# Attention of a two-layer graph network: scores of two heads at a time, alternating between the row halves of the array

## The chip, the cores and the metric

The kernel runs on one core of one Trainium2 chip. The metric is the device time in microseconds; the times of the runs shown are 4495.94, 4510.7 and 4512.44 us, with the median 4510.7. All arithmetic is fp32. In the profile PE is TensorE's matrix product, PEld its load of the stationary operand, DVE is VectorE, ACT is ScalarE, POOL is GpSimd and SP is SyncE.

## The reference

Sixteen graphs of 1024 nodes with 256 channels share one adjacency matrix. Layer 0 is an attention whose queries come from a weighted graph product, layer 1 a graph convolution with two batch norms. Cut to what matters:

```python
h = relu(layernorm(x))
Wg = adj * A_s(mean over channels of h)          # per graph, 1024 x 1024
q = relu(einsum(h^T, Wg) * para)                 # 4 heads of 64 channels
k, v = split(h @ kv_w)
attn = softmax(q @ k^T * scale)                  # per graph and head, 1024 x 1024
x = x + attn @ v
h = relu(layernorm(x))
agg = A_hat @ h                                  # normalised adj + I
y = relu(batchnorm(agg @ W1^T + b1))             # over all graphs and nodes
x = x + batchnorm(y @ W2^T + b2)
```

## The kernel before

The first part of the kernel runs graph by graph. `pre(b)` makes queries, keys and values of graph b; `post(b)` is layer 1 of graph b up to the statistics of its first batch norm, with `y` going to DRAM. The second part, after all graphs, applies the batch norms and the second product; the change doesn't touch it.

Queries and keys lie in SBUF with channels on the partitions: two tiles of 128 partitions for 256 channels, so that each tile holds two heads, one on partitions 0 to 63 and the other on 64 to 127 (tile `k`, first partition `r0`). Attention is cut into units of one graph, one head and 128 queries: 16 x 4 x 8 = 512 units, in the order graph, head, query tile.

`scores` of a unit makes two products of 64 rows by 512 keys (line 262) into one PSUM tile of two banks (`sc`, from a pool of two tiles), takes the row maximum on VectorE (line 270), the exponential with its sum on ScalarE (line 272, into `p`), and the reciprocal of the sum (line 273). A product of 64 rows uses only the half of the array whose rows belong to those partitions. `attend` of a unit transposes `p` on TensorE in eight blocks (line 283, `tp`), copies each four blocks to SBUF, the first on ScalarE (line 288) and the second on VectorE (line 290), multiplies with the values (line 295, `po`, eight products), and adds the scaled result to `x` on VectorE (line 303).

In the program, `scores` of unit i+1 stands ahead of `attend` of unit i. Between the units stands other work: `background(b)` gives out, in 46 pieces spread over the units of graph b, `post(b-1)` (products `pa` line 319 and `py` line 332, normalisation `h_b` line 154 on ScalarE) and then `pre(b+1)` (transposes `cbp` line 108 and `htp` line 198, graph weights `w` lines 176 to 184 on ScalarE and VectorE, products `pg` line 213, `pk` line 231, `pv` line 247). Graph 0 has the preparation of the adjacency matrix in place of `post`; the last graph has no `pre`, so the later part of its attention stands alone. When a graph's pieces run out, attention runs alone too.

The order on each engine is fixed when the program is built, and it isn't the program's: the framework moves instructions ahead of others that it expects to wait. So a score product can stand among the transposes and products of an earlier unit. At run time each engine works through its list in order; TensorE's weight loads may run beside the product in front of them.

## Time and profile before

| | |
|---|---|
| times of the runs shown | 4495.94, 4510.7, 4512.44 us (median 4510.7) |
| span of the profiled execution | 4498.9 us |
| its own time, beside the span | the page gives the span alone; the median of the runs is 11.8 us above it |
| mean granted TensorE clock | 0.96 |
| attention with its background | 80 to 4104 us of the span |
| score products `sc`, line 262, busy | 1146.5 us in 2048 passes |
| weighted sums `po`, line 295, busy | 1086.4 us in 8192 passes |
| transposes `tp`, line 283, busy | 564.3 us in 4096 |
| DMA | mean 33 GB/s |

A product of fp32 operands stands in the trace as two passes, a transpose as one. Lengths of TensorE's records overlap (each reaches to its modelled end), so what a pass holds the engine for is read from one start to the next. A value in brackets on a timeline's line is idle time of that engine just before it and what ended it. The granted clock is 1.00 or 0.50 in any short stretch; a mean between the two says how much of the stretch was spent at each.

### The profile page before, as it was taken

How to read it: one execution, taken by the hardware profiler on the slowest of the kernel's cores; microseconds unless marked ns; L12 is line 12 of the kernel's file. 1: busy time of each engine (PE TensorE's matmuls, PEld its weight loads, DVE VectorE, ACT ScalarE, POOL GpSimd, SP SyncE). 2: the span in 40 equal slices, each digit the busy share in tenths (PEclk: the TensorE clock that was granted, in tenths of full speed). 3: DMA queues.
4: the chain of work that ended last, by engine and by line, in shares of the span. 5: the costliest groups of instructions: out<-in, count | busy, mean ns of one | idle time of the engine just before them, and what ended most of it. 6: DMA issues, size and time to landing. Idle time of an engine off the chain costs nothing.

```text
span 4498.9 us, 48480 instructions
## 1 busy us (share of the span) xinstructions
PE 4345.1 (97%) x19848; PEld 2752.5 (61%) x19848; DVE 1842.1 (41%) x3314; ACT 1705.9 (38%) x3075; POOL 159.9 (4%) x237
## 2 busy tenths in 40 slices
PE   6999999999999999999999999999999999999994
PEld 5765757566665757566665756666575756655443
DVE  5343334344443444444433434344333444333344
ACT  4434334252433434343433434243433425232443
POOL 0000000000000000000000000000000000000001
PEclk9799999999999999999999999999999999999997
DMA  2000010000000000000001000000000000000537
GB/s 112 1 19 19 1 38 1 29 10 19 19 10 29 1 33 6 29 10 19 19 1 38 1 29 10 22 17 15 24 1 36 3 29 10 10 19 29 191 140 271
DMA packets 44236, 148.34 MB, mean 33 GB/s; under 512 B 3824, under 2 KB 20720, under 8 KB 35824
## 3 DMA queue, kind: packets, MB, share of 16 engines
q1 hardware_dynamic: 27120, 78.13, 4.8%
q0 software_dynamic: 16896, 67.12, 3.9%
q8 instruction: 157, 2.57, 0.2%
q14 instruction: 63, 0.52, 0.0%
HBM read 78.13 MB, written 67.11 MB: 32 GB/s over the span
## 4 chain that ended last, share of the span: by engine, by line
PE 90%; ACT 5%; DMA 2%; issue 1%; DVE 1%; POOL 0%; POOLq 0%; SPq 0%; DVEq 0%; ACTq 0%
PE po L295 23%; PE sc L262 21%; PE tp L283 10%; PE pg L213 10%; PE pa L319 10%; PE pz L413 5%; PE py L332 5%; PE pk L231 2%; PE pv L247 2%; ACT w L176 2%; ACT h_b L154 1%; DMA xo<-x_d 1%; DMA out_dram<-xo 1%; ACT p L272 1%; PE htp L198 1%
## 5 line engine op out<-in xcount | busy, mean ns | idle before, releaser
L295 PEld LDWEIGHTS po<-v,pt 128*128 128x128 f32 x8192 | 1015.9, 199 | 450.9 <-ACT pt L288 306.1
L262 PE MATMUL sc<-k,q 64*128 64x512 f32 x2048 | 1146.5, 649 | 35.6 <-ACT p L272 35.6
L295 PE MATMUL po<-v,pt 128*128 128x64 f32 x8192 | 1086.4, 285 | 14.9 <-ACT pt L288 8.1
L288 ACT COPY pt<-tp 128x512 f32<-128x512 f32 x512 | 297.9, 582 | 1308.5 <-PE tp L283 1306.9
L270 DVE TENSOR_REDUCE smx<-sc 128x1 f32<-128x1024 f32 x512 | 625.7, 1222 | 366.0 <-PE sc L262 360.0
L283 PEld LDWEIGHTS tp<-ident,p 128*128 128x128 f32 x4096 | 455.3, 143 | 310.3 <-issue 164.3
L272 ACT ACTIVATE p<-sc,smx 128x1024 f32<-128x1024 f32 x512 | 568.7, 1111 | 166.2 <-DVE smx L270 111.4
L283 PE MATMUL tp<-ident,p 128*128 128x128 f32 x4096 | 564.3, 279 | 0.8 <-ACT p L272 0.8
L262 PEld LDWEIGHTS sc<-k,q 64*128 64x128 f32 x2048 | 314.8, 187 | 337.5 <-issue 262.9
L213 PE MATMUL pg<-w,h_a 128*128 128x256 f32 x2048 | 500.1, 400 | 8.5 <-DVE q L221 5.4
L319 PE MATMUL pa<-aht,h_b 128*128 128x512 f32 x1024 | 481.4, 629 | 4.1 <-ACT h_b L154 4.1
L303 DVE SCALAR_TENSOR_TENSOR x<-po,smx,x 128x64 f32<-128x64 f32 x512 | 145.1, 283 | 769.4 <-PE po L295 769.4
L213 PEld LDWEIGHTS pg<-w,h_a 128*128 128x128 f32 x2048 | 400.4, 201 | 63.4 <-issue 5.4
L290 DVE COPY pt<-tp 128x512 f32<-128x512 f32 x512 | 349.1, 682 | 55.0 <-PE tp L283 55.0
L319 PEld LDWEIGHTS pa<-aht,h_b 128*128 128x128 f32 x1024 | 204.7, 204 | 245.9 <-issue 240.3
L176 ACT ACTIVATE w<-cbc,csum 128x256 f32<-128x256 f32 x512 | 227.1, 499 | 163.0 <-PE pg L213 162.5
L332 PE MATMUL py<-at,w 128*128 128x512 f32 x512 | 250.0, 608 | 0.0
L413 PE MATMUL pz<-yin,w 128*128 128x512 f32 x512 | 221.9, 597 | 11.1 <-ACT yin L407 11.1
L340 ACT ACTIVATE y<-py,vec 128x512 f32<-128x512 f32 x128 | 87.9, 687 | 308.3 <-PE py L332 211.3
L273 DVE RECIPROCAL smx<-smx 128x1 f32<-128x1 f32 x512 | 82.7, 161 | 270.6 <-ACT p L272 268.5
L326 DVE COPY at<-pa 128x512 f32<-128x512 f32 x64 | 44.3, 692 | 345.0 <-PE pa L319 345.0
L221 DVE TENSOR_TENSOR q<-pg,para_sb 128x256 f32<-128x256 f32 x128 | 54.0, 424 | 316.3 <-PE pg L213 315.2
(71 smaller groups left out, 2213.7 us busy)
## 6 DMA issues: line engine op xcount, KB each, us to landing
y_d<-y POOLq DMA_DIRECT2D x128, 256.0 KB, 2.7
yin<-y_d SPq DMA_DIRECT2D x32, 1024.0 KB, 4.8
x<-in_x_dram SPq DMA_DIRECT2D x16, 1024.0 KB, 5.5
x_d<-x POOLq DMA_DIRECT2D x16, 1024.0 KB, 4.1
xo<-x_d SPq DMA_DIRECT2D x16, 1024.0 KB, 7.7
out_dram<-xo POOLq DMA_DIRECT2D x16, 1024.0 KB, 7.1
adj_sb<-in_adj_dram SPq DMA_DIRECT2D x1, 4096.0 KB, 15.2
aht<-in_adj_t_dram SPq DMA_DIRECT2D x1, 4096.0 KB, 25.1
```

Of the source, the lines that this page charges most:

```text
L176: nc.scalar.activation(w[:, t, :], cbc[:, q * QW : (q + 1) * QW], AF.Abs, bias=csum[:, t : t + 1], scale=-1.0,)
L213: nc.tensor.matmul(pg[:, :QW], h[:, t, k * P : (k + 1) * P], w[:, t, :], start=(t == 0), stop=(t == NT - 1),)
L262: nc.tensor.matmul(sc[:, g * FB : (g + 1) * FB], qs[b][k][r0 : r0 + HD, t * P : (t + 1) * P], ks[b][k][r0 : r0 + HD, g * FB : (g + 1) * FB ...
L270: nc.vector.tensor_reduce(sm[:, 0:1], sc, AX.X, ALU.max, negate=True)
L272: nc.scalar.activation(pr, sc, AF.Exp, bias=sm[:, 0:1], accum_out=sm[:, 1:2])
L283: nc.tensor.transpose(tp[:, j * P : (j + 1) * P], pr[:, m * P : (m + 1) * P], ident)
L288: nc.scalar.copy(pt, tp)
L290: nc.vector.tensor_copy(pt, tp)
L295: nc.tensor.matmul(po[:, :HD], pts[g][:, j * P : (j + 1) * P], vs[b][:, m, hd * HD : (hd + 1) * HD], start=(m == 0), stop=(m == NT - 1),)
L319: nc.tensor.matmul(pa, h[:, t, k * P : (k + 1) * P], aht[:, t, g * FB : (g + 1) * FB], start=(t == 0), stop=(t == NT - 1),)
L332: nc.tensor.matmul(py, w1[:, k, j * P : (j + 1) * P], at[:, k, :], start=(k == 0), stop=(k == CC - 1),)
L413: nc.tensor.matmul(pz, w2[:, j, k * P : (k + 1) * P], y[:, j, :], start=(j == 0), stop=(j == HC - 1),)
```

## The change

Attention works on pairs of heads: a unit is one graph, one channel tile `k` (that is, two heads) and 128 queries, 256 units in all. `scores` makes four products in the order head A first half, head B first half, head A second half, head B second half; the two heads lie on different row halves of the array and go into two PSUM tiles (the pool still has two, so a pair takes both). The maximum, exponential and reciprocal of A and then of B follow. In the main loop both `attend` of a unit now come first and `scores` of the next unit after them; before, the next `scores` came first. The tile `p` is from a pool of three buffers in place of two. The 46 pieces of background are spread over 16 units of a graph in place of 32. Comments were dropped.

```diff
-        def scores(b, hd, t):
-            k, r0 = divmod(hd * HD, P)
-            sc = ps_sc.tile([P, N], F32, tag="sc", name=f"sc_{b}_{hd}_{t}")
+        def scores(b, k, t):
+            sc = [
+                ps_sc.tile([P, N], F32, tag="sc", name=f"sc_{b}_{k}_{t}_{e}") for e in range(2)
+            ]
             for g in range(NH):
-                nc.tensor.matmul(
-                    sc[:, g * FB : (g + 1) * FB],
-                    qs[b][k][r0 : r0 + HD, t * P : (t + 1) * P],
-                    ks[b][k][r0 : r0 + HD, g * FB : (g + 1) * FB],
-                    start=True,
-                    stop=True,
-                )
-            sm = p3.tile([P, 3], F32, tag="smx", name=f"smx_{b}_{hd}_{t}")
-            nc.vector.tensor_reduce(sm[:, 0:1], sc, AX.X, ALU.max, negate=True)
-            pr = p2.tile([P, N], F32, tag="p", name=f"p_{b}_{hd}_{t}")
-            nc.scalar.activation(pr, sc, AF.Exp, bias=sm[:, 0:1], accum_out=sm[:, 1:2])
-            nc.vector.reciprocal(sm[:, 2:3], sm[:, 1:2])
-            return pr, sm
+                for e in range(2):
+                    r0 = e * HD
+                    nc.tensor.matmul(
+                        sc[e][:, g * FB : (g + 1) * FB],
+                        qs[b][k][r0 : r0 + HD, t * P : (t + 1) * P],
+                        ks[b][k][r0 : r0 + HD, g * FB : (g + 1) * FB],
+                        start=True,
+                        stop=True,
+                    )
+            made = []
+            for e in range(2):
+                sm = p3.tile([P, 3], F32, tag="smx", name=f"smx_{b}_{k}_{t}_{e}")
+                nc.vector.tensor_reduce(sm[:, 0:1], sc[e], AX.X, ALU.max, negate=True)
+                pr = p3.tile([P, N], F32, tag="p", name=f"p_{b}_{k}_{t}_{e}")
+                nc.scalar.activation(
+                    pr, sc[e], AF.Exp, bias=sm[:, 0:1], accum_out=sm[:, 1:2]
+                )
+                nc.vector.reciprocal(sm[:, 2:3], sm[:, 1:2])
+                made.append((pr, sm))
+            return made
...
-        units = [(b, hd, t) for b in range(B) for hd in range(HEADS) for t in range(NT)]
-        per_graph = HEADS * NT
+        units = [(b, k, t) for b in range(B) for k in range(CC) for t in range(NT)]
+        per_graph = CC * NT
...
-            following = scores(*units[i + 1]) if i + 1 < len(units) else None
-            attend(*unit, *made)
-            made = following
+            attend(b, 2 * k, t, *made[0])
+            attend(b, 2 * k + 1, t, *made[1])
+            made = scores(*units[i + 1]) if i + 1 < len(units) else None
```

More of the change, by code (lines that the diff above doesn't have):

```diff
@@ L362, in gnn_two_layers_kernel @@
         bg = iter(())
-        for i, unit in enumerate(units):
+        for i, (b, k, t) in enumerate(units):
             u = i % per_graph
             if u == 0:
-                bg = background(unit[0])
+                bg = background(b)
             for _ in range((u + 1) * PIECES // per_graph - u * PIECES // per_graph):
```

## The prediction

> **What bounds the kernel now.** I read the page first, then the chain of waits by line, then the timeline of TensorE, ScalarE and VectorE in a stretch of attention alone, then windows with the granted clock.

> ```profile
> span 4498.9 us, 48480 instructions
> PE 4345.1 (97%) x19848; PEld 2752.5 (61%) x19848; DVE 1842.1 (41%) x3314; ACT 1705.9 (38%) x3075; POOL 159.9 (4%) x237
> PE 90%; ACT 5%; DMA 2%; issue 1%; DVE 1%; POOL 0%; POOLq 0%; SPq 0%; DVEq 0%; ACTq 0%
> L262 PE MATMUL sc<-k,q 64*128 64x512 f32 x2048 | 1146.5, 649 | 35.6 <-ACT p L272 35.6
> ```

> TensorE is the bound, and the score products `sc` are its dearest line. Each fp32 product shows as two passes: 1,024 products, 2,048 records.

> ```profile
> 1343.60 1.12 PE L262 MATMUL sc<-k,q 64*128 64x512 f32 x2
> 1344.66 1.09 PE L283 MATMUL tp<-ident,p 128*128 128x128 f32 x8
> 1345.68 1.12 PE L262 MATMUL sc<-k,q 64*128 64x512 f32 x2
> 1344.77 1.22 DVE L270 TENSOR_REDUCE smx<-sc 128x1 f32<-128x1024 f32 x1
> 1346.08 1.11 ACT L272 ACTIVATE p<-sc,smx 128x1024 f32<-128x1024 f32 x1
> 1349.72 1.09 PE L283 MATMUL tp<-ident,p 128*128 128x128 f32 x8
> 1350.74 1.98 PE L262 MATMUL sc<-k,q 64*128 64x512 f32 x4
> 1354.34 2.05 PE L262 MATMUL sc<-k,q 64*128 64x512 f32 x2 [1.63 <-ACT p L272]
> ```

> Columns: start, length, engine, count. Two prices are here. A product (x2) holds TensorE 1.06 us until the next line starts (1343.60 to 1344.66); x4 against x2 is 1.98 against 1.12, so a pass is 0.43 us, and 1.06 - 0.86 = 0.20 is fixed; the start before a run comes 0.09 late as well (start to start, transpose to transpose is 0.11, transpose to score 0.20). So each unbroken run of score passes costs 0.29 us on top. And the softmax's latency: the score's run ends at 1344.66, the maximum runs 1344.77 to 1345.99, the exponential 1346.08 to 1347.19, so that with another 0.1 for the hand-over the transposes of that head can start 2.6 us after its last score pass. They start at 1349.72: 2.5 us to spare.

> ```profile
> 108.50:163.10 54.60, 52.24 (x170) 35.43 (x170) 16.83 (x27) 22.88 (x40) 0.00 (x0) 0.50 0.00 1
> 1334.00:1344.20 10.20, 10.20 (x58) 6.62 (x56) 5.85 (x13) 3.58 (x6) 0.00 (x0) 1.00 0.00 0
> 1350.70:1354.40 3.70, 2.07 (x6) 0.73 (x5) 1.99 (x3) 3.70 (x9) 0.00 (x0) 1.00 0.04 8
> 1354.40:1364.60 10.20, 10.20 (x24) 6.02 (x25) 3.92 (x20) 1.46 (x3) 0.88 (x2) 0.50 0.30 102
> 1494.30:1497.70 3.40, 2.60 (x7) 0.85 (x5) 1.88 (x3) 3.40 (x5) 0.00 (x0) 1.00 0.00 0
> 1497.70:1504.60 6.90, 6.83 (x24) 5.68 (x24) 3.83 (x4) 1.73 (x4) 0.00 (x0) 0.51 0.01 2
> 4004.00:4102.00 98.00, 98.00 (x543) 63.97 (x542) 47.03 (x88) 35.44 (x60) 0.00 (x0) 1.00 0.00 1
> ```

> Columns: window, its length, busy PE, PEld, DVE, ACT, POOL, granted clock. This decides the forecast. Attention alone keeps the full clock for 98 us when PE never idles (4004). But an idle of 1.63 us (1352.7 to 1354.3) or of 0.80 (in 1494.3:1497.7) among score passes is followed by half clock; an idle of 0.52 at 1518 was not. And once at half, attention alone does not bring it back: 108.5 to 163.1 stays at 0.50 although PE is busy 52.24 of 54.60 us. It came back there after

> ```profile
> 157.81 3.67 PE L295 MATMUL po<-v,pt 128*128 128x64 f32 x16
> 161.28 1.91 PE L198 MATMUL htp<-ident,h_a 128*128 128x128 f32 x8
> ```

> that is, no score pass for 5 us; elsewhere after full-width `pa` or `pg` products.

> **The change part by part.** Same products, reductions, exponentials and copies; only order, names and one more buffer for `p` (SBUF; no time). From the order in which the built kernels' instructions stand on TensorE:

> Runs. Before, the 1,024 score products stand in 885 unbroken runs; after, in 725. 160 x 0.29 = -46 us.

> Overlap. Of up to 768 places where a product could follow one of the other row half, the build kept 269; the rest are split by transposes and `po`. Within a product the two passes share a half, so only the second's first pass can lie beside the first's last: at most 0.43 each. No row shows two halves at work at once, so the saving lies between 0 and 269 x 0.43 = 115. I take 0.32: starts that wait for a weight load alone (transposes) are 0.11 apart, 0.43 - 0.11. -86 us. [...]

> Cover lost. The program now issues both attends first and the next scores last, and the build uses score products as filler: in a pair without other work the order is tp(A), sc(A) half, po(A), tp(B), sc(B) half, po(B), sc(A) half, sc(B) half, then at once tp(A) of that pair. Between A's last pass and its transposes lies one product: 0.86 + 0.09 exit, less 0.32 if overlapped = 0.63 us. Against 2.6 that is an idle of 2.0 us. Where other work stands there (`pa`, `py`, `pg`, `pk`, `pv`) it is covered. 60 places are bare: per graph 1 to 14 the sixth pair of the first two heads (there four small transposes cover 0.44, idle 1.5), the last pair, and the first of the next; 4 at graph 0's end and 11 pairs in graph 15. Head B waits 1.2 longer but has tp(A), a score and po(A) before it. Queued behind the waiting transposes is all of TensorE; `po`, its VectorE update and the copies wait with it, nothing else ends later. At each graph's start ScalarE also has `h_b` (eight of 0.5 us, 4.04 in all) ahead of the copy `pt` for which `po` waits: about 2 us more.

> The clock. Each of these idles is longer than the 0.80 that was followed by half clock. So from each bare place to the next full-width work TensorE runs at half, and work there costs double:
> - 14 sixth pairs: 30.1 us of TensorE work to the first `pg`; the fall comes some 2 us late, 2 us of `pg` are caught: +30, +1.5 idle, x14 = 441.
> - 15 graph ends: 18.9 us less four overlaps = 17.6; -2, +3 of `pa`; +2.0 and +1.3 idle; less what is there now (1.63 idle, and 10.2 or 3.4 us of half clock, 3.4 lost on average): 17 x 15 = 255.
> - last graph, 11 pairs: a pair is four products 3.43 + three runs 0.87 + 16 transposes 1.74 + 16 `po` products 3.58 - 0.32 = 9.3; doubled, with 2.6 - 2 x 0.63 = 1.3 idle, 19.9 against 10.1 (2 x 5.06) now: 9.8 x 11 = 108.
> - graph 0, three pairs more: 29.

> 833 in all. In the new order `po` runs straight into eight transposes, like the return at 163; by that one case I take a fifth back: 666. The cost lies between 0 (clock holds) and 833.

> [...]

> Sum on the profiled execution: 4499 - 46 - 86 + 666 = 5033. The median of the runs, 4510.7, stands 12 above the span: 5045.

> **Rivals.**
> 1. The clock holds (ends not slower). Then only idles count: 46 x 2.0 + 14 x 1.5 = 113, the `h_b` copies 15 x 2 = 30, less 15 x 1.63 = 24 gone: 4499 - 132 + 119 + 12 = 4498. For: idle of 0.52 left it alone. Against: 0.80 and 1.63 did not. It decides if the bare idles stay under some 0.5 us, that is, if the softmax were ready 1.5 us sooner than its rows say.
> 2. The halves do not overlap: the change does not do what it says. 86 come back, 60 idles are 0.32 shorter, some of the lost overlap is doubled (10): 5045 + 77 = 5120. For: no row shows overlap. Against: separate rows, separate banks.
> 3. The clock comes back at the first small cluster, half of the 833: 4499 - 132 + 416 + 12 = 4795. For: the return at 163. Against: half clock had then lasted 54.6 us, where it moves in steps of 3.4 (stretches of 3.4, 6.9 and 10.2).
> 4. Nothing is given back: 5045 + 167 = 5212.

> **How the numbers follow.** Forecast 0.45 (own range 4900 to 5200), rival 1 0.16, 2 0.15, 3 0.16, 4 0.08. About 0.5% is what a measurement of this kernel can tell from no change. Rival 1 lies about it, half faster, half same: faster 0.08, same 0.08, slower 0.84. The range runs from 4560, which leaves out rival 1, to 5280, above rival 4.

> **What would show it.** TensorE's mean clock near 0.83 instead of 0.96; transposes `tp` waiting for the exponential in some 60 places, 1.3 to 2 us each (now 0.8 us in all); half clock in most of the last graph's attention; a first pass of head B starting about 0.1 us after the last pass of A, where they stand side by side, instead of 0.43. I am wrong if the idles are there at full clock, or if the transposes do not wait at all.

## The result, and the profile after

The changed kernel takes 4724.06 us in the median of three runs (4710.84 to 4732.29), against 4510.7 before: the ratio is 1.0472, with a 95% interval of 1.0423 to 1.0521. It is slower, as forecast, and the time lies inside the range, but below the 4900 to 5200 us of the likeliest case: it grew by 213 us where that had 534. Where executions of one kernel lie more than 1.5% apart, the ratios below leave the upper ones out; the traces of e3, e6 and e12 are of such upper ones.

The page of the kernel after, with the lines that answer to those shown of before (busy time on the engines, the shares of the chain that ended last, and the groups of the score products and the transposes):

```profile
span 4708.8 us, 48087 instructions
PE 4424.3 (94%) x19848; PEld 2908.1 (62%) x19848; DVE 1846.5 (39%) x3314; ACT 1702.3 (36%) x3075; POOL 159.8 (3%) x237
PE 84%; ACT 8%; DVE 4%; DMA 2%; issue 2%; POOL 0%; POOLq 0%; SPq 0%; ACTq 0%; DVEq 0%
L266 PE MATMUL sc<-k,q 64*128 64x512 f32 x2048 | 1050.2, 750 | 2.0 <-ACT p L278 2.0
L292 PE MATMUL tp<-ident,p 128*128 128x128 f32 x4096 | 648.4, 306 | 142.9 <-ACT p L278 142.2
```

TensorE is still the bound, but its share of the chain fell from 90% to 84%, and ScalarE's and VectorE's grew: the softmax now stands on the chain. The score products are busy for 1050 us, 96 less than before, although 369 us of that are now at half clock, against 56 before. And the transposes, which waited 0.8 us in all, wait 142.2 us for the exponential. In the view of waits (line, what it waited for: total, times, longest) these are 59 places; the first line is of before, the other two of after:

```profile
PE tp L283 <- ACT p L272: 0.8, 1, 0.8
PE tp L292 <- ACT p L278: 142.2, 59, 2.6
PE po L304 <- ACT pt L297: 11.7, 38, 1.1
```

The timeline of TensorE in one bare stretch, graph 2's end (start, length, engine, operation, count, idle before it):

```profile
870.15 1.13 PE L266 MATMUL sc<-k,q 64*128 64x512 f32 x4
873.83 1.09 PE L292 MATMUL tp<-ident,p 128*128 128x128 f32 x8 [2.55 <-ACT p L278]
874.85 1.12 PE L266 MATMUL sc<-k,q 64*128 64x512 f32 x2
875.90 2.00 PE L304 MATMUL po<-v,pt 128*128 128x64 f32 x16
877.74 1.04 PE L292 MATMUL tp<-ident,p 128*128 128x128 f32 x8
878.71 1.12 PE L266 MATMUL sc<-k,q 64*128 64x512 f32 x2
879.76 2.00 PE L304 MATMUL po<-v,pt 128*128 128x64 f32 x16
881.69 1.13 PE L266 MATMUL sc<-k,q 64*128 64x512 f32 x4
885.37 1.21 PE L292 MATMUL tp<-ident,p 128*128 128x128 f32 x8 [2.55 <-ACT p L278]
```

Two things are to be seen. The order is the one forecast: transposes, a product, weighted sum for A, the same for B, then a product of each head, then A's transposes, which wait. And `x4`, two whole products of different row halves (four passes), holds 1.13 us, the same as `x2`, one product (1.12): the second product costs nothing. The starts within such a run are about 0.01, 0.53 and 0.01 us apart: first pass of A, first of B, second of A, second of B.

Windows of the kernel after (window, length, busy PE, PEld, DVE, ACT, POOL, granted clock, DMA share, GB/s): two sixth pairs, each with the work that follows, and the last graph's bare attention:

```profile
706.00:708.50 2.50, 0.54 (x5) 0.30 (x4) 2.50 (x3) 1.28 (x3) 0.00 (x0) 1.00 0.01 3
708.50:766.80 58.30, 58.30 (x186) 39.51 (x187) 18.21 (x28) 24.76 (x44) 0.00 (x0) 0.50 0.00 1
979.90:982.50 2.60, 0.67 (x6) 0.42 (x4) 2.48 (x3) 1.23 (x3) 0.00 (x0) 1.00 0.00 0
982.50:1040.00 57.50, 57.19 (x335) 41.68 (x336) 29.17 (x46) 35.94 (x65) 0.00 (x0) 1.00 0.00 1
4128.00:4252.00 124.00, 108.71 (x367) 74.89 (x366) 30.20 (x58) 22.82 (x40) 0.00 (x0) 0.50 0.00 0
4128.00:4326.00 198.00, 168.56 (x604) 117.92 (x602) 52.47 (x102) 37.42 (x66) 2.46 (x3) 0.55 0.01 5
```

The same idle of 1.96 us stands in both sixth pairs. After the one, TensorE ran at half clock for 58 us with no idle at all; after the other it kept the full clock. In the last graph the clock is at half for nearly all of the bare attention.

By stages, cut at the first product `pa` of each graph, and with the time at half clock from the clock record:

| stage | before, us (at half) | after, us (at half) | difference |
|---|---|---|---|
| start to graph 1's first `pa` | 335.8 (63.5) | 378.0 (170.7) | +42 |
| the 14 periods from there to graph 15's first `pa` | 3584 (215) | 3667 (683) | +83 |
| last graph, to its `post`'s first `pa` | 194.9 (7.2) | 280.6 (180.2) | +86 |
| to the start of `pz`, the second part's product | 55.2 (10.8) | 55.0 (10.6) | 0 |
| from there to the end | 329.0 (68.3) | 327.7 (60.0) | -1 |

Before, a period was 254.5 or 257.5 us. After, seven periods in which the sixth pair's idle was not followed by half clock are 248.7 to 252.4 us, faster than before, and the seven in which it was are 264.3 to 278.3.

The whole adds up. A covered product saves 0.86 us (two passes of 0.43); by the order of TensorE's instructions 224 are covered: -193. The 160 score runs fewer were put at -46 (not measured by itself). TensorE's idle times over 0.2 us grew from 145 to 265 us: +121. Time at half clock grew from 364.8 to 1104.5 us; without the idle that lies in it (32.9 and 92.8), work at half clock grew by 680 us, and half of that is lost: +340. The sum is +222; the spans differ by +210. (That work takes about twice as long at half clock is read from the prediction's lines: a product holds TensorE 1.99 us from 1354.34, and 1.06 at full clock. Idle and lost clock taken out of both spans, the work fell by 251 us, where the first two terms give 239.)

### The profile page after: what moved, and what is told of

Same layout as the page of the kernel before. It is cut to its first block, busy times and chain, and to the rows that moved or that the text cites. A ratio compares the mean times of both kernels' runs of the same rounds, so it can differ in the third digit from the quotient of the medians.

```text
span 4708.8 us, 48087 instructions
## 1 busy us (share of the span) xinstructions
PE 4424.3 (94%) x19848; PEld 2908.1 (62%) x19848; DVE 1846.5 (39%) x3314; ACT 1702.3 (36%) x3075; POOL 159.8 (3%) x237
## 4 chain that ended last, share of the span: by engine, by line
PE 84%; ACT 8%; DVE 4%; DMA 2%; issue 2%; POOL 0%; POOLq 0%; SPq 0%; ACTq 0%; DVEq 0%
PE po L304 24%; PE sc L266 20%; PE tp L292 11%; PE pa L328 9%; PE pg L213 6%; PE py L341 5%; PE pz L422 5%; ACT p L278 3%; DVE smx L276 3%; PE pv L247 2%; ACT w L176 2%; PE pk L231 1%; ACT w L183 1%; DMA out_dram<-xo 1%; PE htp L198 1%
## 5 line engine op out<-in xcount | busy, mean ns | idle before, releaser
L304 PEld LDWEIGHTS po<-v,pt 128*128 128x128 f32 x8192 | 1127.5, 218 | 473.3 <-ACT pt L297 211.4
L304 PE MATMUL po<-v,pt 128*128 128x64 f32 x8192 | 1198.4, 305 | 19.9 <-ACT pt L297 11.7
L266 PE MATMUL sc<-k,q 64*128 64x512 f32 x2048 | 1050.2, 750 | 2.0 <-ACT p L278 2.0
L292 PE MATMUL tp<-ident,p 128*128 128x128 f32 x4096 | 648.4, 306 | 142.9 <-ACT p L278 142.2
L292 PEld LDWEIGHTS tp<-ident,p 128*128 128x128 f32 x4096 | 548.8, 163 | 305.1 <-ACT p L278 214.9
L213 PE MATMUL pg<-w,h_a 128*128 128x256 f32 x2048 | 476.6, 387 | 8.5 <-DVE q L221 5.4
L266 PEld LDWEIGHTS sc<-k,q 64*128 64x128 f32 x2048 | 285.8, 216 | 176.8 <-issue 153.7
L328 PEld LDWEIGHTS pa<-aht,h_b 128*128 128x128 f32 x1024 | 194.9, 194 | 241.6 <-issue 236.0
L341 PEld LDWEIGHTS py<-at,w 128*128 128x128 f32 x512 | 90.8, 189 | 149.6 <-issue 94.0
L422 PEld LDWEIGHTS pz<-yin,w 128*128 128x128 f32 x512 | 97.9, 192 | 135.0 <-issue 124.4
L184 DVE SCALAR_TENSOR_TENSOR w<-w,adj_sb 128x2048 f32<-128x2048 f32 x64 | 146.4, 2288 | 50.9 <-ACT w L183 50.4
```

Source lines behind the costliest of these rows:

```text
L213: nc.tensor.matmul(pg[:, :QW], h[:, t, k * P : (k + 1) * P], w[:, t, :], start=(t == 0), stop=(t == NT - 1),)
L266: nc.tensor.matmul(sc[e][:, g * FB : (g + 1) * FB], qs[b][k][r0 : r0 + HD, t * P : (t + 1) * P], ks[b][k][r0 : r0 + HD, g * FB : (g + 1) * ...
L292: nc.tensor.transpose(tp[:, j * P : (j + 1) * P], pr[:, m * P : (m + 1) * P], ident)
L304: nc.tensor.matmul(po[:, :HD], pts[g][:, j * P : (j + 1) * P], vs[b][:, m, hd * HD : (hd + 1) * HD], start=(m == 0), stop=(m == NT - 1),)
L328: nc.tensor.matmul(pa, h[:, t, k * P : (k + 1) * P], aht[:, t, g * FB : (g + 1) * FB], start=(t == 0), stop=(t == NT - 1),)
L341: nc.tensor.matmul(py, w1[:, k, j * P : (j + 1) * P], at[:, k, :], start=(k == 0), stop=(k == CC - 1),)
```

## The experiments

The theory after the result: the change gains some 190 us by overlap, and loses more by idle places, which cost 121 us themselves and some 340 through the half clock that follows them; both ends of it come from the order, in which a pair's scores stand last before their own transposes. Rivals: the time is lost in the pairing itself (the weight loads, the PSUM tiles, the buffers), or the clock falls for another reason than the idle.

**Scores between the two attends (e1).** Put back some cover: the next pair's scores ahead of B's `attend`.

```diff
             attend(b, 2 * k, t, *made[0])
+            following = scores(*units[i + 1]) if i + 1 < len(units) else None
             attend(b, 2 * k + 1, t, *made[1])
-            made = scores(*units[i + 1]) if i + 1 < len(units) else None
+            made = following
```

> Pairs as in the change, but the next pair's scores stand between the two attends in the program. In the built order 240 products ride beside another and only one head's transposes have less than 2.5 us of TensorE work between them and their last score pass (60 in the change). Theory (the loss is the idle in bare places and the half clock that follows it; the pairing itself gains): the idles and their half clock go, the overlap stays, TensorE's work by the trace's prices is 254 us below the kernel before: about 4260 us (4220 to 4330), mean clock 0.95 or more. Rival (pairing itself lowers the clock or is worth nothing): 4500 us or more.

Measured: 4816 us (4779 to 4869), ratio 1.0634 [1.0555, 1.0713], with 1155 us at half clock. The forecast of a gain fell. Its waits on TensorE:

```profile
PE sc L266 <- ACT p L278: 252.2, 180, 3.0
PE tp L292 <- ACT p L278: 2.5, 1, 2.5
```

The transposes hardly wait any more. In their place 180 score products wait for the same exponential. The reading: it has to be done with the PSUM tiles first, because a pair takes both `sc` tiles of the pool, so no score of the next pair can start before this pair's softmax is through. Before, one unit took one of two tiles, and the other was free for the next. The idle was moved, not covered. That the tiles are the reason rests on the releaser in these lines and on the size of the pool; no run gave the pool more tiles.

**Pairs in one row half (e2).** The same order on TensorE and on ScalarE, instruction for instruction in the two traces (VectorE's differs in places), but the pair is two query tiles of one head, so that the two row halves are not both at work.

```diff
-                    r0 = e * HD
-                    nc.tensor.matmul(sc[e]..., qs[b][k][r0 : r0 + HD, t * P : (t + 1) * P], ...
+                    nc.tensor.matmul(sc[e]..., qs[b][k][r0 : r0 + HD, (2*t+e) * P : (2*t+e+1) * P], ...
...
-        units = [(b, k, t) for b in range(B) for k in range(CC) for t in range(NT)]
+        units = [(b, hd, t) for b in range(B) for hd in range(HEADS) for t in range(NT // 2)]
...
```

> The change with a pair made of two query tiles of one head, so both lie on the same row half; the order on TensorE is the changed kernel's, instruction for instruction. Theory (each of 224 products that stand beside the other half costs nothing now and 0.86 us without the overlap): 224 x 0.86 = 193 us more, the 60 idles 0.86 us shorter = 52 less, some half clock less: about 4840 us (4760 to 4930), starts of neighbouring score passes 0.43 apart in place of 0.01. Rival (overlap hidden anyway, because TensorE waits after it): within 25 us of the changed kernel.

Measured: 4759 us (4746 to 4769), ratio 1.054 [1.0484, 1.0596]. Its timeline at the place that answers to 870 us of the changed kernel, and its waits:

```profile
875.26 1.98 PE L266 MATMUL sc<-k,q 64*128 64x512 f32 x4
878.93 1.09 PE L292 MATMUL tp<-ident,p 128*128 128x128 f32 x8 [1.70 <-ACT p L278]
PE tp L292 <- ACT p L278: 70.7, 59, 1.7
```

Four passes hold 1.98 us instead of 1.13, so the overlap does come from the two row halves; and the idle that follows is 1.70 instead of 2.55, shorter by just the 0.85 saved. The 59 waits sum to 70.7 us against 142.2. The overlap is worth only 35 us net (39 by the two spans). Of the 193 us gained, 103 come back as idle: TensorE's idle times over 0.2 us are 163 us here and 265 with overlap. Of that difference 72 us lie at these transposes, and most of the rest at copies and activations that `po`, `pv` and `py` wait for. Another 34 go into the clock (943 us of work at half here, 1012 with overlap). That leaves 56 where the spans have 39; the 17 between them stay unexplained.

**The new order without pairs (e3).** The kernel before, with `attend` ahead of the next `scores`.

```diff
-            following = scores(*units[i + 1]) if i + 1 < len(units) else None
             attend(*unit, *made)
-            made = following
+            made = scores(*units[i + 1]) if i + 1 < len(units) else None
```

> The kernel before (single heads) with the one change that attend stands ahead of the next scores in the program. Theory (the order makes bare places, the pairs make them deep): 691 runs of score passes against 885, so 194 x 0.29 = 56 us less; 30 bare places of about 0.9 us = 27 us more, some half clock: 4470 to 4560 us. Rival (the order alone is the whole cost of the change): 4650 us or more.

Measured: 4437.5 us (4369 to 4460), ratio 0.9737 [0.9641, 0.9833]: faster than before, and below what was expected. Its waits:

```profile
PE tp L283 <- ACT p L272: 26.4, 31, 0.9
```

Single heads keep one `sc` tile free, so the order by itself loses nothing; the transposes wait in 31 places, but only 0.9 us each (26.4 us in all), and the 35.6 us that scores waited for the exponential before are gone. So it isn't the order alone that makes the change slow, but the order with pairs, whose idles are 2 to 3 times as long.

**Filling the bare places (e4, e5, e7, e8).** If the idle is the cause, then useless products put into it must make the kernel faster, although they are more work. The filler writes a PSUM tile that nobody reads.

```diff
             made = scores(*units[i + 1]) if i + 1 < len(units) else None
+            if b == B - 1 and u >= 4 and made:
+                fill = ps_mm.tile([P, FB], F32, tag="mm", name=f"fill_{i}")
+                for j in range(3):
+                    nc.tensor.matmul(fill, w1[:, 0, :P], aht[:, j, :FB], start=j == 0, stop=j == 2)
```

This is e4, in the last graph alone. In e5 the condition is `u >= 11 if b == 0 else u >= 4 if b == B - 1 else u in (4, 14, 15)`, 58 of the 60 bare places. e7 is e4 with 64 rows (`[:HD]`) of both operands, e8 is e4 with one product in place of three. The 260 us in what was expected of these two are for the last graph's stage.

> The change, and in the last graph three full-width products of 128 x 512 (2.57 us) that nobody reads, in each of 11 bare places, where TensorE now idles 2.55 us. The computation is the same; only work is added. Theory (the clock, not the idle itself, is the larger part): idle and added work are equal, so at full clock a pair lasts 11.5 us as it would with the idle, but the clock stays full and the last graph's attention takes about 127 us in place of 193: about 4660 us (4640 to 4685). Rival (the idle is the cost and the clock follows something else): 4720 us or more.

> The change with three full-width products of 128 x 512 that nobody reads (2.57 us) in 58 of its 60 bare places. The computation is the same, 174 products are added. Theory (the half clock after the bare places is what makes the change slow): the idle of 142 us turns into 149 us of work, so at full clock nothing is gained or lost, and the time at half clock falls from 1104 us to about 400, that is 350 us less: about 4385 us (4330 to 4450), faster than the kernel before. Rival (the work at half clock is slow for another reason, or other idles take over): 4600 us or more.

> The change, and in the last graph's 11 bare places three products of 64 rows by 512 (2.57 us, nobody reads them) in place of full-width ones. [...] Rival (only full-width work holds the clock): 260 us or more, as unfilled (281).

> The change, and in the last graph's 11 bare places one full-width product of 128 x 512 (0.86 us, nobody reads it), so that 1.7 us of idle are left. [...] Rival (an idle of 1.7 us is enough for the fall, as 1.63 was in the kernel before): 260 us or more.

| | time, us | last graph's stage (at half) |
|---|---|---|
| the changed kernel | 4724 | 280.6 (180.2) |
| e4, three products | 4665.6 (4631 to 4688), ratio 1.0322 [1.025, 1.0393] | 210.6 (5.8) |
| e7, three of 64 rows | 4619.4, one run | 208.1 (1.6) |
| e8, one product | 4713.8, one run | 226.2 (45.3) |
| e5, three at 58 places | 4360.7 (4351 to 4375), ratio 0.9677 [0.9619, 0.9735] | 209.0 (1.5) |

The last graph of e4, in a window that answers to that from 4128 of the changed kernel:

```profile
4110.00:4300.00 190.00, 188.56 (x963) 116.57 (x961) 76.98 (x140) 54.62 (x94) 4.41 (x8) 1.00 0.03 12
```

The clock there is 1.00 and PE busy for 188.56 of 190 us. 33 useless products made the stage 70 us shorter; in 58 places, 174 of them made the kernel 363 us faster than the changed one and 3.2% faster than before. In e5's trace the transposes wait for the exponential once, and the time at half clock is 244 us in place of 1104 (mean clock 0.972 in place of 0.883):

```profile
core 0: 4367.6 us, clock 0.972
PE tp L292 <- ACT p L278: 2.5, 1, 2.5
```

That is the theory's main point shown: the idles, through the clock, cost more than the overlap gains. e7's stage, with 64 rows in the filler, has 1.6 us at half clock where e4's has 5.8, so the filler need not be of full width here; both stages, 208.1 and 226.2 us, lie below the 260 of the rivals. In e8 the 0.86 us of filler leave 45.3 us at half of the 180.2: what remains of an idle there is about 1.7 us at full clock, an estimate from 2.55 less 0.86 (its waits have 11 places and 15.1 us more than e4's).

The changed kernel, e4, e7 and e8 are the same program up to the last graph, and yet their spans (4708.8, 4686.2, 4617.7 and 4712.0 us) do not differ as that stage does: e4's is only 23 us shorter, e8's 3 us longer. The periods tell why: the sixth pair's idle was followed by half clock in 7, 9, 7 and 10 of 14 graphs, in this order, at some 20 us each (272.8 us for a period with it and 251.2 without, in the changed kernel's means).

**Alternating single heads (e6, e9).** A way to have overlap without pairs: e3 with the units in the order graph, channel tile, query tile, head, so that neighbours lie in different row halves.

```diff
-        units = [(b, hd, t) for b in range(B) for hd in range(HEADS) for t in range(NT)]
+        units = [(b, 2 * k + e, t) for b in range(B) for k in range(CC) for t in range(NT) for e in range(2)]
```

> Single heads, attend ahead of the next scores, and the units alternate between the two heads of a channel tile. 75 products then stand beside one of the other row half in the built order. Theory: 75 x 0.86 = 64 us less than single heads with attend first (4437), 25 us more idle, some half clock: about 4400 us (4340 to 4470). Rival (overlap leaves idles that lower the clock, so it is worth nothing): 4437 us or more.

Measured: 4923 us (4849 to 4952), ratio 1.0821 [1.0722, 1.092], with 1515 us at half clock: the slowest of all. The theory had put the gain of the overlap on top of e3 and left out what e2 had shown: that it bares the idle. Waits and timeline of e6:

```profile
PE tp L283 <- ACT p L272: 52.9, 31, 2.5
```

```profile
1442.50 1.99 PE L262 MATMUL sc<-k,q 64*128 64x512 f32 x6
1446.24 1.09 PE L283 MATMUL tp<-ident,p 128*128 128x128 f32 x8 [1.75 <-ACT p L272]
```

Six passes in 1.99 us, where three products of one half hold 2.84 (at 1515.05 us of the kernel before): the overlap took the cover, and e3's idle of 0.9 us became 1.75. In e3 most idles were not followed by half clock (5 of the 30 of 0.84 and 0.90 us were); here the idle of 1.69 us early in a graph was in 14 of 15 graphs, for 72 us each (116 in the last), and that of 1.75 us at a graph's end in 10 of 14, for 27 us each. To see that it was these two, e9 puts two useless products at each of them:

```diff
+            if u == 9 and unit[0] > 0 or (u == 29 and 0 < unit[0] < B - 1):
+                fill = ps_mm.tile([P, FB], F32, tag="mm", name=f"fill_{i}")
+                for j in range(2):
+                    nc.tensor.matmul(fill, w1[:, 0, :P], aht[:, j, :FB], start=j == 0, stop=j == 1)
```

> The alternating single heads, and two full-width products that nobody reads (1.71 us) in the two bare places of each graph. The computation is the same, work is added. Theory (4923 was slow because two idles of 1.7 us in each graph are followed by half clock): the idles are gone, the time at half clock falls from 1515 to about 300 us, worth some 600, against 80 us more TensorE work in the new order: about 4400 us (4330 to 4480). Rival (alternating heads are slow in themselves): 4800 us or more.

Measured: 4407 us (4400 to 4408), ratio 0.9769 [0.9735, 0.9802], with 245 us at half clock in place of 1515. 58 useless products at 29 places made the kernel 516 us faster.

**Spreading the background (e10, e11, e12).** The pieces are given out as if a graph had 46 of them, and run out early (graphs 1 to 14 have 37, counted in the kernel), which leaves the places at the graphs' ends bare. With 42 (e10, on the changed kernel) and 44 (e11, on e3), real work stands there instead, and in e10 the idle of 1.96 us at the sixth pair is gone too.

```diff
-        PIECES = 46
+        PIECES = 42
```

> The change with one number altered: the background is spread as if it had 42 pieces, not 46, so that it lasts to the last pair of a graph. No work is added or taken. In the built order 28 bare places are left of 60: the sixth pair's and the last pair's are gone, the one at each graph's start stays, 9 of 11 in the last graph. Theory: the sixth pairs' idle (28 us) and half clock (7 falls of some 47 us, 165 us of work), the last pairs' idle (38 us) and a part of the rest go, TensorE's work is 21 us less: about 4420 us (4360 to 4500), below the kernel before. Rival (the falls move to other places): 4600 us or more.

> Single heads with attend ahead of the next scores, and the background spread as if it had 44 pieces. No work is added. 16 bare places of 0.9 us idle in place of 30, but 845 runs of score passes in place of 691. Theory: 45 us more from the runs, less half clock (the falls of 40 to 50 us in every second graph go): 4390 us (4340 to 4450). Rival (idles of 0.9 us do not matter for the clock): 4437 + 45 - 14 = 4470 us or more.

Measured: e10 4356 us (4340 to 4377), ratio 0.9661 [0.9615, 0.9707]; e11 4330 us (4329 to 4346), ratio 0.9612 [0.9569, 0.9655]. Both are faster than before with no work added. In e10 the periods are 237.4 to 238.6 us with 3.4 to 6.8 us of half clock each; in e11 nearly all are 245.4 with none. So where neither loses much of the clock, pairs are 7 to 8 us a graph faster than singles. (In e10 the idle of 2.55 us at each graph's start is still there, but the half clock that follows lasts only those 3.4 to 6.8 us, where the first stretch at a graph's end of the changed kernel lasted 20 to 24 us at 13 of 14 ends.) But e10's last graph has nothing to spread: 270.9 us, 170 of them at half clock, against e11's 191.0. That asks for pairs in graphs 0 to 14 and single heads in the last (e12).

```diff
-        units = [(b, k, t) for b in range(B) for k in range(CC) for t in range(NT)]
+        for b in range(B):
+            ess = [(0, 1)] if b < B - 1 else [(0,), (1,)]
+            of = [(b, k, t, es) for k in range(CC) for es in ess for t in range(NT)]
...
+            PIECES = 42 if b < B - 1 else 44
...
+            for j, e in enumerate(es):
+                attend(b, 2 * k + e, t, *made[j])
```

> Pairs with the background spread as for 42 pieces in graphs 0 to 14, and single heads with attend ahead of the next scores in the last graph, where attention stands alone and the pairs had nine bare places. No work is added. Theory: graphs 1 to 14 keep their 237 to 239 us, the last graph's stage takes some 195 us as with single heads, in place of 271: about 4280 us (4240 to 4320). Rival (the clock falls in the last graph for another reason): 4340 us or more.

Measured: 4292 us (4257 to 4321), ratio 0.9488 [0.9412, 0.9564], the fastest of all, near the time expected. The last graph takes 193.9 us, as with singles, and the other periods 236 to 242. Whether 42 or 44 pieces would help the kernel before, without any other edit, was not tried.

## Why the prediction was right or wrong

*Direction and mechanism: right; two terms of the sum were mis-sized.* The larger miss is the clock, the smaller the overlap; both made the forecast too slow. "Cover lost" and "the clock" were named as what decides, and the fillers (e4, e5, e9) show both: the idle of the transposes sits in 59 places where 60 were forecast (the places that the prediction lists add up to 57), and without it most of the half clock goes. The mean clock fell to 0.883 (forecast 0.83).

*Overlap, -86: mis-sized, -193 measured.* The step that failed is "within a product the two passes share a half, so only the second's first pass can lie beside the first's last: at most 0.43 each". It took for granted that the two passes of a product follow one another before the next product starts. They don't: first passes of both heads start together, then both second passes, and the whole product of 0.86 us is covered. In the trace most such starts side by side are 6 to 7 ns apart, at full clock and at half (four are about 50). Instead of 269 covered passes at 0.32 us there are 448 (224 products of two) at 0.43.

*Idle at a bare place, 2.0 us: right place, 2.55 measured.* The same error: 0.63 us of cover was left in the sum, and the overlap took all of it (e2, without overlap, idles 1.70). In the sixth pairs the forecast was 1.5 and the trace has 1.96.

*Softmax latency 2.6 us: right*; it is 2.55 from the end of the scores to the transposes.

*`h_b` ahead of `pt`, about 30 us: too much.* All 38 waits of `po` on that copy sum to 11.7 us (before, 8.1 in 17); the one behind `h_b` in the period shown is 0.91 us and not 2.

*The clock, +666 with its idle: mis-sized, about 461 measured* (121 of idle and 340 of work at half clock). The step that failed is "So from each bare place to the next full-width work TensorE runs at half". It was wrong at both ends. Not every idle was followed by half clock: seven of the fourteen in the sixth pairs (1.96 us) kept the full clock, which the prediction had named as a sign of being wrong; of the 20 idles of 2.55 us at full clock 18 were followed by half. And the clock did not wait for full-width work: six of the seven stretches that did begin there ended before the first `pg`, and at 13 of the 14 graph ends the clock was back before the first `pa`. By its parts:

- Sixth pairs, forecast 441 before the deduction: it had all 14 fall, at some 30 us each besides the idle. Seven fell, at about 22 us each: some 150. The idle itself was 27 us in 14 places, where 21 were put. The forecast took one idle of 0.80 us that had been followed by half clock as proof that any longer one would be. The stretches were 31 to 58 us long (mean 47) where 60 was put.
- Graph ends, forecast 255: the first half clock there lasted 20 to 24 us at 13 of 14 ends and not some 35 (at five ends another 10 us came after it). At those 13 the clock was back after eight transposes and four to eight overlapped score passes; what brought it back was not tested.
- Last graph, forecast 108: 86 measured. Its price was right in sum: 19.9 us a pair forecast at half clock, and by the next two lines of the timeline after 19.45. But that is two errors that cancel: 2.55 us of it are idle and 16.90 work, where 1.3 and 18.6 were put.

```profile
4203.64 1.97 PE L292 MATMUL tp<-ident,p 128*128 128x128 f32 x8 [2.55 <-ACT p L278]
4223.09 1.97 PE L292 MATMUL tp<-ident,p 128*128 128x128 f32 x8 [2.55 <-ACT p L278]
```

- Graph 0, forecast 29: the first stage is 42 us longer.

Overlap was 107 us better than forecast and the clock 205 us: 312 of the 324 us by which the predicted span (5033) missed.

*The rivals.* The first, that the clock holds, was wrong for this kernel; but where the clock does hold its 4498 is too high: with the idles filled, e5 takes 4361. The second, that the halves don't overlap, is refuted by 1.13 against 1.12 us; and e2 priced it at 35 us, not 77. The third, that half of the 833 is paid (4795), came nearest in size, and for its reason only in small part: three of the seven stretches in the sixth pairs (31, 41 and 41 us) ended where sixteen `po` passes run into eight transposes, like the return at 163. But the same order stands in every pair of the last graph's 123 us at half clock, and only the last one ended them; and the larger part is that the clock did not fall in half of the sixth pairs. The fourth, that nothing is given back (5212), missed by more than the forecast.

## What to carry to other kernels

An overlap on the bound engine also takes away the cover of whatever waits behind it (here 103 of the 193 us gained came back as idle): count the time saved and the wait laid bare together, place by place, and then ask what the idle does to the clock. Where a pair took both tiles of the PSUM pool, the next pair's scores waited for the softmax (e1: 180 places, 252.2 us); single units with one tile free were the better form in the last graph, where no other work could be put in between (191.0 us in e11 against 270.9 in e10). Where an idle costs clock, spread real work into it first (one constant here was worth 7.8% of the changed kernel's time), and use a few useless products as the quick test of whether the idle is the cause.
